# All work of border tiles five to eight in one conditional block over five engines

## The chip, the cores and the metric

The kernel runs on one core of one Trainium2 chip. The core has a matrix engine (TensorE, PE in the profile), a vector engine (VectorE, DVE), a scalar engine (ScalarE, ACT), a general engine (GpSimd, POOL) and an engine that mostly issues transfers (SyncE, SP). Each runs its own program in order; semaphores join them. Sixteen DMA engines move data. The metric is the device time of one execution in microseconds (us), lower is better; the number to be predicted is the median of several runs.

## What is computed

For 16 batches of 512 tokens with 512 features, the reference adds to `x` a small network over six normalised views of it, of which three take their scale and shift from tables by token, and three add a row per batch:

```python
h = _ln(x, pw_g[pathway_ids], pw_b[pathway_ids])
h = _ln(h, cp_g[compartment_ids], cp_b[compartment_ids])
t = _ln(x, tm_g[time_steps], tm_b[time_steps])
m = x + _mlp_ln(memory_state, ...)[:, None, :]
n = x + _mlp_ln(noise_state, ...)[:, None, :]
r = x + _mlp_ln(resource_state, ...)[:, None, :]
s = _ln(x, ms_g[scale_type], ms_b[scale_type])
cat = jnp.concatenate([w[0] * h, w[1] * t, w[2] * m, w[3] * n, w[4] * r, w[5] * s], axis=-1)
return x + _mlp_ln(cat, int_W1, int_b1, int_W2, int_b2, int_g, int_be)
```

## The kernel before

The tokens are sorted by the group of their table entries, so that most quarters of a window share one set of weights; the 8192 tokens are 16 windows of 512, each of four tiles of 128 rows. For a window, POOL gathers the rows of `x` (`gx`, into one of three buffers `xbs[0..2]`), the table rows (`gh`, `gc`) and an additive row per token (`ga`, from the DRAM table `rows_2`); ACT and DVE make the normalised rows (`xs`, `xe`, `xp`, `xm`, `nv`, `f1`, `fs`, `f2`, `fn`); DVE turns them (`tx`, `tv`, `th`), SP spreads the turned blocks (`sX`, `sV`, `sH`) into the operands `cats["X"]`, `cats["V"]`, `cats["H"]`; PE multiplies them by the weights (`lX`, `lV`, `lH` in the first windows). `lV.w.g` uses the weights `vs` that DVE updates in `bd.w.g` where the group changes. The buffers `xbs` go round: window 0 is in `xbs[2]` (`sh.0.j` adds a vector to its rows there), window 1 in `xbs[0]`, and `gx.2.j` gathers window 2 into `xbs[1]`.

Where a group's border falls inside a tile, a correction row is needed. Such rows are collected in border tiles of 128 rows, numbered k = 0 to 7, tiles one to four (k = 0 to 3) in the set `e0`, tiles five to eight (k = 4 to 7) in `e1`. How many rows there are is known only at run time, so every step of a border tile stands in a conditional of its own, on one engine: the tokens' numbers (`gt.1.j`, `tk.1`, `xa.1`), the gather of the rows (`gx.e1.j`), their sums (`xs.e1.j`, `xe.e1`, `xp.e1`, `xm.e1`), a gather of differences (`gr.e1.j`), normalisation and product (`nv.e1.j`, `mt.e1.j`), PE's transposition (`ey.k`), ACT's copy (`ez.k`), POOL's gather of what is added to (`ea.k`, tile `adde`), PE's product (`ex.k`), DVE's sum (`ee.k`) and SP's store to `rows_2` (`eo.k`). `rf.k` writes a filling row block to `rows_2` where the tile is empty, from `xbs[0]`. If the condition doesn't hold, the engine of a step walks over it, and raises the semaphores that its instructions would have raised; the other engines meet one branch.

The list `ORDER`, written out by hand, sets the order of all pieces up to the middle of window 2; each engine's program is the pieces' instructions on it in that order. Behind it the strings `WINDOW` and `LAST` do the same for the rest. In `ORDER` the pieces of tiles five to eight stand among those of tiles one to four and of window 1: the gathers and `rf.4` to `rf.7` early, `ey`, `ez`, `ea`, `ex`, `ee`, `eo` between `gx.2.3`, `xp.1`, `xm.1`, `lH.0.1` and `ga.0.1`.

Of the kernel before, what the change touches and what calls it, by code (L numbers as in the profile page):

```python
# [15 lines left out]
P = 128  # L16
# [5 lines left out]
    wk.1.3 wk.1.1 dk g4 wk.1.2 lt wk.1.0 h2.0 se ax pk cv sz g6 xs.0.0 scl fg wk.2.3 h2.2 he.0 sp.0.0 g5 h2.1  # L22
    pwi wk.2.2 xs.0.2 he.1 cg lo xt.0.0 he.2 lw bx lh by xt.0.1 gh.0.0 fl.3 xv.0.0 cw eh.1 xs.0.3 gc.0.0 xs.0.1
    xe.0 xt.0.3 wm.4 vd.0 kd xt.0.2 eh.0 wl.4 ac gh.0.2 xp.0 xm.0 tt nv.0.1 gt.0.0 eh.2 f1.0.0 nv.0.2 cs xv.0.3
    fs.0.0 gt.0.3 f1.0.2 dp gt.0.2 gt.0.1 cp fv.0.0 vt.0.1 fl.2 tk.0 xv.0.1 vt.0.2 va.1 cn vv.0.1 fl.4 tb wm.3
    nv.0.3 gc.0.2 gt.1.2 gt.1.0 vd.1 gt.1.3 va.0 ct ca wk.2.1 fl.1 wk.2.0 dc wm.2 do nv.0.0 gx.e0.0 vv.0.2
    gx.e0.1 rf.2 gx.e0.3 xv.0.2 sp.0.1 rf.6 rf.5 rf.1 xs.e0.0 f2.0.0 vt.0.0 vt.0.3 fs.0.2 f2.0.2 cm xs.e0.1 cr
    gt.1.1 gx.e0.2 lX.0.1 fp.0.0 fn.0.0 va.2 xs.e0.2 ht.0.0 gr.e0.0 rp1 gr.e0.1 xs.e0.3 rp.0 rp.1 rc.1 fv.0.2
    bd.0.0 bd.0.1 gh.0.1 vv.0.3 rc.0 wm.0 rf.0 lX.0.0 xe.e0 rf.7 tk.1 xp.e0 gx.e1.2 xm.e0 gx.e1.0 fp.0.2 rp2
    rf.4 hv.0.0 rf.3 fl.0 nv.e0.0 lX.0.2 mt.e0.0 gx.1.0 nv.e0.2 xa.0 nv.e0.1 mt.e0.1 ey.1 ey.0 vv.0.0 fn.0.2  # L30
    ez.0 wm.1 f1.0.1 gx.1.2 fs.0.1 gx.e1.1 gr.e0.2 ht.0.2 xa.1 hv.0.2 mt.e0.2 fv.0.1 xs.e1.1 ro.1 ro.0 ea.0
# [10 lines left out]
    fs.1.0 f1.1.1 fv.1.0 ha.0.1 hs.0.1 gc.1.1 ga.0.0 ha.0.3 ha.0.2 f2.1.0 tz.0.1 bd.1.1 ha.0.0 gx.2.0 sV.1.3
    sV.1.2 hs.0.2 kb.0.1 lV.1.0 hs.0.3 hs.0.0 tz.0.2 sX.1.3 tz.0.0 tz.0.3 gx.2.1 kb.0.0 sZ.0.1 xs.2.3 wq sh.0.3
    xs.2.0 xs.2.1 fs.1.1 sZ.0.0 sZ.0.2 ga.1.1 ga.1.2 sh.0.0 fp.1.0 fn.1.0 th.1.0 fv.1.1 zs.0.0 fp.1.1 lV.1.1
    m7.1.1.1 m7.1.0.1 q7.0.0.1 zs.0.1 zs.0.2 xe.2 q7.0.0.7 f2.1.1 fn.1.1 tx.2.2 th.1.1 gh.2.0 q7.0.0.2 xp.2
    kf.0.0 q7.0.0.5 q7.0.0.6 ku.0.0 sf.0.0 kz.0.3 kf.0.1 sZ.0.3 sp.1.2 kb.0.3 sp.1.3 bd.1.3 sh.1.2 tx.2.1
    q7.0.1.1 q7.0.1.2 sf.0.1 zs.0.3 zs.0.4 zs.0.5 lV.1.3 r1.1.1 kf.0.2 sf.0.2 tx.2.3 xm.2 nv.2.3 sl.0.0 ga.1.0
    sH.1.0 sH.1.3 nv.2.1 q7.0.1.5 tv.2.3 kf.0.3 sH.1.1 q7.0.0.3 nv.2.2 f1.2.0 q7.0.1.7 q7.0.0.4 tv.2.1 zs.0.6
    fs.2.0 nv.2.0 sh.1.1 zs.0.7 tv.2.2 sl.0.1 sf.0.3 sh.1.3 q7.0.1.6 m7.1.0.2 q7.0.1.4 q7.0.1.3 tv.2.0 fv.2.0
    r1.1.0 gh.2.1 lq.0.1 lq.0.0 sH.1.2 tx.2.0 bd.1.2 u1.1.1 u3.1.1 lV.1.2 u2.1.1 ku.0.1 m7.1.1.5 gc.2.0 sl.0.2  # L50
    sl.0.3 u1.1.0 u2.1.0 ga.1.3 lq.0.2 lq.0.3 f1.2.1 m7.1.1.4 m7.1.0.5 lv.0 m7.1.1.2 m7.1.0.6 r5.1.1 vd.2 f2.2.0
    sV.2.0 sp.2.0 lp.0 fp.2.0 fs.2.1 sp.2.1 fn.2.0 lb.0.0 lb.0.2 lb.0.3 po.0.0 gc.2.1 po.0.3 u4.1.0 u3.1.0
    fv.2.1 fp.2.1 r5.1.0 gx.3.0 r2.1.0 sV.2.1 sX.2.2 sV.2.3 sV.2.2 sX.2.0 m7.1.1.6 lb.0.1 u4.1.1 m7.1.0.7 gx.3.3
    bd.2.1 sX.2.1 r2.1.1 m7.1.0.3 m7.1.0.4 th.2.0 bd.2.0 f2.2.1 ha.1.0 r3.1.0 ha.1.1 m7.1.1.7 gh.2.2 gx.3.1
    gx.3.2 hs.1.1 po.0.1 fn.2.1 r3.1.1 th.2.1 gh.2.3 ha.1.3 m7.1.1.3 sh.1.0 sX.2.3 tz.1.1 hs.1.0 po.0.2 tz.1.0
    hs.1.3
# [38 lines left out]
def kernel(ctx: ExitStack, tc: tile.TileContext, a: dict, out: bass.AP):  # L95
# [190 lines left out]
    def x_sums(st, j):  # L286

        if st["w"] in BY_DVE:
            if "sums" not in st:
# [4 lines left out]
        if "sums" not in st:
            st["sums"] = small.tile([P, 3, NJ], F32, tag="sums", name="sums")
            if "n" in st:
                nc.vector.memset(st["sums"], 0.0)
# [1076 lines left out]
    def flip_extra(k):
        at_["px", k] = pt = ps.tile([P, NC, P], F32, tag="p", name=f"px{k}")
        r = ext[k // Q].pop(("r", k % Q))
        with tc.If(at_["some", 0][k] > 0):
            for c in range(NC):
                nc.tensor.transpose(pt[:, c], r[:, c * P : (c + 1) * P], ident)
# [8 lines left out]
    def extra(k):
        if ("pe", k) not in at_:
            at_["pe", k] = psum(f"pe{k}")  # L1390
        pe = at_["pe", k]
        with tc.If(at_["some", 0][k] > 0):
# [8 lines left out]

    def extra_end(k):
        with tc.If(at_["some", 1][k] > 0):
            nc.vector.tensor_add(at_["adde", k], at_["pe", k], at_["adde", k])
# [164 lines left out]
```

## Time and profile before

| | us |
|---|---|
| median of three runs (lowest, highest) | 915.65 (914.73, 918.04) |
| the profiled execution's own time | 914.96 |
| its span, first to last instruction | 913.2 |
| PE busy (share) | 884.2 (97%) |
| DVE busy (share) | 750.5 (82%) |
| POOL busy (share) | 676.7 (74%) |
| ACT busy (share) | 525.0 (57%) |

The profile has a page with shares, slices and groups, and views of the trace behind it. A row of the timeline has the start in us from the span's start, the busy time in us, the engine, the line of the code, the operation, what it writes and reads, a count of merged instructions, and in square brackets the idle time of the engine before it with what ended it. "PEq" is PE's sequencer (its branches and semaphores), "issue" means that nothing in the profile was waited for. A row of the waits has who waited for whom, the sum in us, the times, the longest. A row of the windows has a stretch, its length, the busy time of PE, PE's weight loads, DVE, ACT and POOL with the number of instructions, the granted clock of PE (1.00 is full), the share of the DMA engines, and GB/s. A row of SP shows when it issued transfers, not when they landed.

### The profile page before, as it was taken

Reading aid. Unit: us, or ns where it says so; the run is one execution under the profiler, and the core shown is the slowest. Engines: PE = TensorE matmul, PEld = TensorE weight load, DVE = VectorE, ACT = ScalarE, POOL = GpSimd, SP = SyncE. Lnnn points to the kernel's source line nnn. Section 1 sums busy time; section 2 is a strip of 40 time slices with the busy share of each in tenths; the row PEclk is TensorE's granted clock in tenths of the full one; section 3 lists DMA queues with packets and bytes.
Section 4 is the critical chain, followed back from the end, with each engine's and each line's share of the span. In section 5 each row is a group of like instructions: output and inputs, shape, how many; then the busy total and the mean of one; then the engine's idle time right before and its main releaser. Section 6 shows DMA issues by size and latency. Waiting matters only on the chain. (4 is left out here: it accounts for less than half of the span.)

```text
span 913.2 us, 13821 instructions
## 1 busy us (share of the span) xinstructions
PE 884.2 (97%) x3615; PEld 642.9 (70%) x3617; DVE 750.5 (82%) x1360; ACT 525.0 (57%) x1263; POOL 676.7 (74%) x726
## 2 busy tenths in 40 slices
PE   6898899999999999999999999999999999999996
...
GB/s 280 247 194 219 204 244 143 169 248 163 254 172 251 184 222 190 192 236 191 245 174 257 168 251 191 216 188 220 210 168 244 190 257 158 245 195 200 151 29 118
DMA packets 88239, 184.36 MB, mean 202 GB/s; under 512 B 24260, under 2 KB 24324, under 8 KB 88156
## 3 DMA queue, kind: packets, MB, share of 16 engines
...
q8 instruction: 30, 0.49, 0.2%
...
## 5 line engine op out<-in xcount | busy, mean ns | idle before, releaser
L417 PE MATMUL p<-vs,catV 128*128 128x512 f32 x512 | 229.7, 592 | 0.7 <-ACT junk L363 0.4
L417 PEld LDWEIGHTS p<-vs,catV 128*128 128x128 f32 x512 | 97.0, 190 | 99.2 <-issue 94.1
L389 ACT ACTIVATE pw<-pw,rsh 128x512 f32<-128x512 f32 x64 | 44.5, 718 | 136.7 <-POOL rsh L385 127.0
L465 PE MATMUL p<-wh__81,catH 128*128 128x256 f32 x480 | 113.4, 379 | 0.9 <-DVE catH L452 0.9
L465 PEld LDWEIGHTS p<-wh__81,catH 128*128 128x128 f32 x480 | 91.0, 190 | 14.0 <-DVE catH L452 1.7
L184 POOL DMA_INDIRECT xbs<-in_x,tok x64 | 74.1, 1158 | 34.8 <-DVE yb L647 18.1
L651 POOL DMA_INDIRECT out<-yb,tok x64 | 70.3, 1098 | 30.3 <-issue 18.3
L184 POOL DMA_INDIRECT cp<-cp_rows,i_cp x64 | 75.3, 1177 | 16.2 <-issue 15.4
L404 POOL TENSOR_TENSOR xbs<-xbs,rows 128x512 f32<-128x512 f32 x64 | 82.5, 1289 | 2.4 <-DMA cp<-cp_rows,i_cp 0.8
L184 POOL DMA_INDIRECT add<-rows,i_add x64 | 66.7, 1042 | 21.0 <-issue 11.7
L488 ACT ACTIVATE add<-add 128x512 f32<-128x512 f32 x64 | 39.9, 630 | 70.0 <-DVE add L485 69.4
L184 POOL DMA_INDIRECT pw<-in_pw,i_pw x64 | 65.1, 1018 | 19.3 <-DVE rH L210 7.5
L396 DVE SCALAR_TENSOR_TENSOR pw<-pw,sumsh,cp 128x512 f32<-128x512 f32 x60 | 55.7, 931 | 10.1 <-DMA cp<-cp_rows,i_cp 8.9
L638 POOL TENSOR_TENSOR rsy<-vey,mhalf 128x4 f32<-128x4 f32 (+1 forms) x16 | 22.0, 1376 | 53.2 <-DVE vey L633 53.2
L625 ACT ACTIVATE junk<-yb 128x512 bf16<-128x512 f32 x64 | 40.2, 629 | 34.4 <-DVE yb L589 16.6
L360 DVE SCALAR_TENSOR_TENSOR pw<-pw,rsx 128x512 f32<-128x512 f32 x64 | 57.5, 899 | 2.3
L385 POOL TENSOR_TENSOR rsh<-veh,mhalf 128x1 f32<-128x1 f32 x64 | 52.6, 824 | 8.4 <-DVE veh L381 6.8
L465 PEld LDWEIGHTS u<-wx__80,catX 128*128 128x128 f32 x240 | 45.6, 190 | 18.1 <-issue 10.0
L465 PE MATMUL u<-wt,catX 128*128 128x256 f32 x240 | 57.0, 381 | 0.9 <-DVE add L476 0.8
L465 PE MATMUL p<-wt,catH 128*128 128x256 f32 x240 | 56.7, 379 | 0.0
L465 PE MATMUL u<-wx__80,catX 128*128 128x256 f32 x240 | 56.5, 379 | 0.0
L465 PE MATMUL u<-wt,ss 128*128 128x256 f32 x240 | 56.4, 379 | 0.0
...
## 6 DMA issues: line engine op xcount, KB each, us to landing
catX<-rX SPq DMA_DIRECT2D x240, 64.0 KB
catV<-rV SPq DMA_DIRECT2D x240, 64.0 KB
catZ<-rZ SPq DMA_DIRECT2D x240, 64.0 KB
catH<-rH SPq DMA_DIRECT2D x240, 64.0 KB
...
```

The costliest lines, as they stand in the source:

```text
L184: nc.gpsimd.indirect_dma_start(dst, None, table, bass.IndirectOffsetOnAxis(ap=idx, axis=0), **kw)
L360: nc.vector.scalar_tensor_tensor(h, h, st["rs"][:, j : j + 1], pw[:, D:], ALU.mult, ALU.add)
L385: nc.gpsimd.tensor_tensor(rs, st.pop(("ve", j)), mhalf[:, :1], ALU.pow)
L389: nc.scalar.mul(pw[:, :D], pw[:, :D], st.pop(("rs", j)))
L396: nc.vector.scalar_tensor_tensor(pw[:, :D], pw[:, :D], st["sh", j][:, 1], cp, ALU.add, ALU.mult)
L404: nc.gpsimd.tensor_add(st["xb"][:, j, :], st["xb"][:, j, :], rows[:, 2, :])
L417: nc.tensor.matmul(st["p1", g], st["c" + blk][:, g, c, :], m[:, c, :], start=(blk == first and c == order[0]), stop=(blk == last and c == ...
L465: nc.tensor.matmul(dst, m[:, c], at_["half1"][k][:, c], start=(k == 1 and c == 0), stop=(c == NC - 1), skip_group_check=True)
L488: nc.scalar.activation(st["add", g], st["add", g], AF.Silu)
L625: nc.scalar.activation(junk, yb[:, j, :], AF.Square, accum_out=st["ssy"][:, j : j + 1])
L638: nc.gpsimd.tensor_tensor(st["rsy"][:, lo:hi], st["vey", lo], mhalf[:, lo:hi], ALU.pow)
L651: nc.gpsimd.indirect_dma_start(out_rows[j], bass.IndirectOffsetOnAxis(ap=tok[:, j, w : w + 1], axis=0), yb[:, j, :], None)
```

## The change

The pieces of tiles five to eight leave their places in `ORDER`. Two new pieces stand for them. `f5` loads the run-time condition for tile five into a register of each of the five engines. `ew`, behind `eo.2 eo.3`, holds all the work of the four tiles in one conditional block over the five engines; its other arm fills the four row blocks, which `rf.4` to `rf.7` did early before. Inside the block the gathers of differences go to `yb`, the normalised rows and the `adde` tiles to `xbs[1]`, the operand to `cats["Z"]`, and one PSUM tile each serves all `px` and all `pe`. The rest of the order is as it was. The core of the diff:

```diff
 ORDER = """
...
-    ... ey.6 bd.0.3 tx.1.0
-    wl.1 xs.1.3 ey.4 ee.2 hv.0.3 ex.3 ee.3 eo.2 eo.3 gr.e1.3 ea.4 xe.1 tx.1.3 mt.e1.3 sh.0.1 gr.e1.1 gh.1.2
-    gx.2.3 ea.7 ea.6 sh.0.2 ey.7 ez.7 ex.7 ea.5 ez.6 nv.e1.1 mt.e1.1 ey.5 sp.0.2 ez.5 xp.1 xm.1 ez.4 ex.4 ex.5
-    ee.5 ex.6 gc.1.3 wl.0 wl.3 gc.1.2 f1.1.3 nv.1.0 nv.1.1 lH.0.1 fs.1.3 lX.0.3 lV.0.3 lH.0.3 eo.5 f1.1.2 ee.6
-    fs.1.2 tv.1.0 ee.7 bd.0.2 f2.1.3 ee.4 eo.4 kz.0.2 lV.0.2 fv.1.2 tv.1.1 f2.1.2 nv.1.3 eo.6 gx.2.2 sX.1.2 eo.7
-    ga.0.1 lH.0.2 fv.1.3 kz.0.1 lH.0.0 ga.0.3 ...
+    ... bd.0.3 tx.1.0 wl.1 xs.1.3 ee.2 hv.0.3 ex.3 ee.3 eo.2 eo.3 ew xe.1 tx.1.3
+    sh.0.1 gh.1.2 gx.2.3 sh.0.2 sp.0.2 xp.1 xm.1 gc.1.3 wl.0 wl.3 gc.1.2 f1.1.3 nv.1.0 nv.1.1 lH.0.1 fs.1.3 lX.0.3
+    lV.0.3 lH.0.3 f1.1.2 fs.1.2 tv.1.0 bd.0.2 f2.1.3 kz.0.2 lV.0.2 fv.1.2 tv.1.1 f2.1.2 nv.1.3 gx.2.2 sX.1.2 ga.0.1
+    lH.0.2 fv.1.3 kz.0.1 lH.0.0 ga.0.3 ...
...
-                with tc.If(at_["some", 3][int(st["w"][1]) * Q + j] > 0):
+                with used(3, int(st["w"][1]) * Q + j):
...
     def rows_first(k):
         to, at = (rows_1, 0) if k == 0 else (rows_2, k - 1)
+        nc.sync.dma_start(to[NB1 + at * P : NB1 + (at + 1) * P, :], xbs[0][:, k % Q])
+
+    def first_of(k):
         with tc.If(at_["some", 4][k] < 1):
-            nc.sync.dma_start(to[NB1 + at * P : NB1 + (at + 1) * P, :], xbs[0][:, k % Q])
+            rows_first(k)
+
+    def used(e, k):
+        return nullcontext() if at_.get("whole") else tc.If(at_["some", e][k] > 0)
+
+    def rest_load():
+        _, at_["rest"] = nc.values_load_multi_w_load_instructions(
+            some[0:1, Q : Q + 1], engines=[mybir.EngineType.PE, mybir.EngineType.DVE, mybir.EngineType.Activation,
+                                           mybir.EngineType.Pool, mybir.EngineType.SP], min_val=0, max_val=2 * P,
+            skip_runtime_bounds_check_because="a comparison's result")
+
+    def rest_extras():
+        js = range(Q)
+        names = [f"gt.1.{j}" for j in js] + ["tk.1", "xa.1"] + [f"gx.e1.{j}" for j in js] + [f"xs.e1.{j}" for j in js]
+        names += ["xe.e1", "xp.e1", "xm.e1"]
+        for j in js:
+            names += [f"gr.e1.{j}", f"nv.e1.{j}", f"mt.e1.{j}", f"ey.{Q + j}", f"ez.{Q + j}"]
+        for j in js:
+            names += [f"ea.{Q + j}", f"ex.{Q + j}", f"ee.{Q + j}", f"eo.{Q + j}"]
+        with tc.If(at_["rest"][0] > 0) as cmp:
+            at_["whole"] = True
+            for n in names:
+                piece(n)
+            at_["whole"] = False
+        with cmp.Else():
+            for j in js:
+                rows_first(Q + j)
...
     def extra_add(k):
-        at_["adde", k] = gp.tile([P, D], F32, tag="add", name=f"adde{k}", bufs=4)
-        with tc.If(at_["some", 3][k] > 0):
+        at_["adde", k] = xbs[1][:, k % Q, :] if at_.get("whole") else gp.tile([P, D], F32, tag="add", name=f"adde{k}", bufs=4)
+        with used(3, k):
             gather(at_["adde", k], rows_1[: NB1 + (P if k else 0), :], add_x[:, k : k + 1])
...
-        "rp": rows_product, "rf": rows_first, ...
+        "rp": rows_product, "rf": first_of, "f5": rest_load, "ew": rest_extras, ...
```

What this moves is seen in each engine's program. A row has the line, the operation, what it writes and reads, the shape, and the semaphores that it waits for: DMASW0 to 7 for POOL's own gathers, DMAHW0 to 7 for the transfers of SP, and one for each engine. Line numbers of the change are its own.

POOL before, from `gh.1.2` (`pw1_2`) and `gx.2.3` (the gather into `xbs1`) on, with the first of the skipped gathers of tiles five to eight behind them:

```order
L184 DMA pw1_2_1414<-in_pw,i_pw_106 128x1024 [waits DMASW6_49,PE_49,Activation_49]
L184 DMA xbs1_90<-in_x,tok_105 128x512 [waits DMASW7_49]
L1399 COMPARE_AND_BRANCH
L184 DMA adde7_1417<-rows_1_76,i_x_539 128x512 [waits DMAHW4_49,DMAHW6_49,DMAHW2_49,DMAHW7_49,DMASW0_49,DVE_49]
L1399 UNCONDITIONAL_BRANCH
L1399 ISA [waits DMASW0_49]
L1399 UNCONDITIONAL_BRANCH
```

The gather `gx.2.3` waits for one earlier gather (DMASW7) there. Two more such skipped gathers, the add of `sh.0.2` and a row of branches stand between it and `xp.1`.

POOL after, from the end of the block's other arm on; `L399` are `sh.0.1` and `sh.0.2`, `rsx_1435` is `xp.1`:

```order
L1378 ISA [waits Pool_49,DMASW4_49,DMASW5_49,DMASW3_49,DMASW6_49,DMASW2_49,DMASW7_49,DMASW1_49,DMASW0_49]
L1378 UNCONDITIONAL_BRANCH
L256 UNCONDITIONAL_BRANCH
L399 TENSOR_TENSOR xbs2_91<-xbs2_91,rows_97 128x512 [waits DMAHW6_49,DMASW1_49]
L179 DMA pw1_2_1426<-in_pw,i_pw_106 128x1024 [waits DMASW0_49,DMASW1_49,PE_49,Activation_49]
L179 DMA xbs1_90<-in_x,tok_105 128x512 [waits DMAHW1_49,DMASW2_49,DVE_49]
L399 TENSOR_TENSOR xbs2_91<-xbs2_91,rows_97 128x512
L308 TENSOR_TENSOR rsx_1435<-vea_1422,mhalf_103 128x4 [waits DVE_49]
L179 DMA cp1_3_1439<-cp_rows_75,i_cp_107 128x512 [waits DMASW4_49,DMASW3_49]
L179 DMA cp1_2_1443<-cp_rows_75,i_cp_107 128x512 [waits DMASW5_49,DMASW4_49]
```

The skipped gathers are gone from between `gx.2.3` and `xp.1`, the arm has one row that waits for all eight queues of gathers, and `gx.2.3` has come to wait for DMAHW1, DMASW2 and DVE.

SP before, in the early part of the program, two of the fills `rf.4` to `rf.7`, each in its own conditional:

```order
L1360 COMPARE_AND_BRANCH
L1361 DMA rows_2_78<-xbs0_89 128x512 [waits DMAHW2_49]
L1360 UNCONDITIONAL_BRANCH
L1360 UNCONDITIONAL_BRANCH [waits DMAHW2_49]
L1360 COMPARE_AND_BRANCH
L1361 DMA rows_2_78<-xbs0_89 128x512 [waits DMAHW3_49]
L1360 UNCONDITIONAL_BRANCH
L1360 UNCONDITIONAL_BRANCH [waits DMAHW3_49]
```

SP after: the same stores from `xbs0` stand as `L1355` in the block's other arm, behind the block's branch, which itself follows the store `eo.3`; `L1434` are the stores `eo.4` to `eo.7` from `xbs1` of the arm with the work.

```order
L1378 COMPARE_AND_BRANCH
L1434 DMA rows_2_78<-xbs1_90 128x512 [waits DMAHW6_49,DVE_49]
L1434 DMA rows_2_78<-xbs1_90 128x512 [waits DMAHW7_49,DVE_49]
L1434 DMA rows_2_78<-xbs1_90 128x512 [waits DMAHW0_49,DVE_49]
L1434 DMA rows_2_78<-xbs1_90 128x512 [waits DMAHW1_49,DVE_49]
L1378 UNCONDITIONAL_BRANCH
L1355 DMA rows_2_78<-xbs0_89 128x512 [waits DMAHW6_49,DMASW3_49]
L1355 DMA rows_2_78<-xbs0_89 128x512 [waits DMAHW7_49,DMASW3_49]
L1355 DMA rows_2_78<-xbs0_89 128x512 [waits DMAHW0_49,DMASW4_49]
L1355 DMA rows_2_78<-xbs0_89 128x512 [waits DMAHW1_49,DMASW2_49]
L1378 UNCONDITIONAL_BRANCH
L256 UNCONDITIONAL_BRANCH
```

The fills have moved from the early part to this place, ahead of the spreads of window 1, and both arms raise DMAHW6, 7, 0 and 1 in this order.

PE before, the last two of the six conditionals between `ex.3` and the product `lH.0.1` (`p1_0_1<-wh`):

```order
L1392 COMPARE_AND_BRANCH
L1394 MATMUL pe5_1473<-wt_83,catX_93 128x512 [waits DVE_49,PE_49,Activation_49]
L1394 MATMUL pe5_1473<-wt_83,catX_93 128x512 x3
L1392 UNCONDITIONAL_BRANCH
L1392 UNCONDITIONAL_BRANCH [waits PE_49]
L1392 COMPARE_AND_BRANCH
L1394 MATMUL pe6_1481<-wt_83,catX_93 128x512 [waits DVE_49,PE_49,Activation_49]
L1394 MATMUL pe6_1481<-wt_83,catX_93 128x512 x3
L1392 UNCONDITIONAL_BRANCH
L1392 UNCONDITIONAL_BRANCH [waits PE_49]
L417 MATMUL p1_0_1_990<-wh__81,catH_94 128x512 [waits DVE_49,Activation_49]
```

PE after, the end of the block's arm with the work, its other arm (`L1378` with a wait for PE itself), and `lH.0.1`:

```order
L1419 MATMUL pe4_1390<-wt_83,catZ_96 128x512 [waits DVE_49]
L1419 MATMUL pe4_1390<-wt_83,catZ_96 128x512 x3
L1419 MATMUL pe4_1390<-wt_83,catZ_96 128x512 [waits DVE_49,Activation_49]
L1419 MATMUL pe4_1390<-wt_83,catZ_96 128x512 x3
L1378 UNCONDITIONAL_BRANCH
L1378 UNCONDITIONAL_BRANCH [waits PE_49]
L256 UNCONDITIONAL_BRANCH
L412 MATMUL p1_0_1_985<-wh__81,catH_94 128x512 [waits DVE_49,Activation_49]
```

The six conditionals, and two ahead of `ex.3`, are gone; one block stands in their place.

More of the change, by code (lines that the diff above doesn't have):

```diff
@@ L1 @@
-from contextlib import ExitStack
+from contextlib import ExitStack, nullcontext
 import concourse.bass as bass
@@ L21 @@
 ORDER = """
[L22 to L31, printed above, removed]
@@ L42 @@
[L42 to L51, printed above, removed]
@@ L52 @@
[L52 to L56, printed above, removed]
+    wk.1.3 wk.1.1 dk g4 wk.1.2 lt wk.1.0 h2.0 se ax pk cv sz g6 xs.0.0 scl fg wk.2.3 h2.2 he.0 sp.0.0 g5 h2.1 pwi
@@ new lines @@
+    wk.2.2 xs.0.2 he.1 cg lo xt.0.0 he.2 lw bx lh by xt.0.1 gh.0.0 fl.3 xv.0.0 cw eh.1 xs.0.3 gc.0.0 xs.0.1 xe.0
+    xt.0.3 wm.4 vd.0 kd xt.0.2 eh.0 wl.4 ac gh.0.2 xp.0 xm.0 tt nv.0.1 gt.0.0 eh.2 f1.0.0 nv.0.2 cs xv.0.3 fs.0.0
+    gt.0.3 f1.0.2 dp gt.0.2 gt.0.1 cp fv.0.0 vt.0.1 fl.2 tk.0 xv.0.1 vt.0.2 va.1 cn vv.0.1 fl.4 f5 tb wm.3 nv.0.3
+    gc.0.2 vd.1 va.0 ct ca wk.2.1 fl.1 wk.2.0 dc wm.2 do nv.0.0 gx.e0.0 vv.0.2 gx.e0.1 rf.2 gx.e0.3 xv.0.2 sp.0.1 rf.1
+    xs.e0.0 f2.0.0 vt.0.0 vt.0.3 fs.0.2 f2.0.2 cm xs.e0.1 cr gx.e0.2 lX.0.1 fp.0.0 fn.0.0 va.2 xs.e0.2 ht.0.0 gr.e0.0
@@ new lines @@
+    rp1 gr.e0.1 xs.e0.3 rp.0 rp.1 rc.1 fv.0.2 bd.0.0 bd.0.1 gh.0.1 vv.0.3 rc.0 wm.0 rf.0 lX.0.0 xe.e0 xp.e0 xm.e0
+    fp.0.2 rp2 hv.0.0 rf.3 fl.0 nv.e0.0 lX.0.2 mt.e0.0 gx.1.0 nv.e0.2 xa.0 nv.e0.1 mt.e0.1 ey.1 ey.0 vv.0.0 fn.0.2
+    ez.0 wm.1 f1.0.1 gx.1.2 fs.0.1 gr.e0.2 ht.0.2 hv.0.2 mt.e0.2 fv.0.1 ro.1 ro.0 ea.0 wl.2 ex.0 gc.0.1 xs.1.0 ez.1
+    ey.2 gh.0.3 wb lV.0.0 f2.0.1 lV.0.1 gr.e0.3 ee.0 fp.0.1 ar nv.e0.3 mt.e0.3 fn.0.1 ht.0.1 f1.0.3 ez.2 xs.1.2 eo.0
+    ey.3 ex.1 gx.1.3 gx.1.1 gc.0.3 fs.0.3 f2.0.3 ea.1 ea.3 gh.1.3 fv.0.3 ex.2 tx.1.2 sp.0.3 fp.0.3 ez.3 xs.1.1 hv.0.1
@@ new lines @@
+    ha.0.1 hs.0.1 gc.1.1 ga.0.0 ha.0.3 ha.0.2 f2.1.0 tz.0.1 bd.1.1 ha.0.0 gx.2.0 sV.1.3 sV.1.2 hs.0.2 kb.0.1 lV.1.0
+    hs.0.3 hs.0.0 tz.0.2 sX.1.3 tz.0.0 tz.0.3 gx.2.1 kb.0.0 sZ.0.1 xs.2.3 wq sh.0.3 xs.2.0 xs.2.1 fs.1.1 sZ.0.0 sZ.0.2
+    ga.1.1 ga.1.2 sh.0.0 fp.1.0 fn.1.0 th.1.0 fv.1.1 zs.0.0 fp.1.1 lV.1.1 m7.1.1.1 m7.1.0.1 q7.0.0.1 zs.0.1 zs.0.2
+    xe.2 q7.0.0.7 f2.1.1 fn.1.1 tx.2.2 th.1.1 gh.2.0 q7.0.0.2 xp.2 kf.0.0 q7.0.0.5 q7.0.0.6 ku.0.0 sf.0.0 kz.0.3
+    kf.0.1 sZ.0.3 sp.1.2 kb.0.3 sp.1.3 bd.1.3 sh.1.2 tx.2.1 q7.0.1.1 q7.0.1.2 sf.0.1 zs.0.3 zs.0.4 zs.0.5 lV.1.3
@@ new lines @@
+    r1.1.1 kf.0.2 sf.0.2 tx.2.3 xm.2 nv.2.3 sl.0.0 ga.1.0 sH.1.0 sH.1.3 nv.2.1 q7.0.1.5 tv.2.3 kf.0.3 sH.1.1 q7.0.0.3
+    nv.2.2 f1.2.0 q7.0.1.7 q7.0.0.4 tv.2.1 zs.0.6 fs.2.0 nv.2.0 sh.1.1 zs.0.7 tv.2.2 sl.0.1 sf.0.3 sh.1.3 q7.0.1.6
+    m7.1.0.2 q7.0.1.4 q7.0.1.3 tv.2.0 fv.2.0 r1.1.0 gh.2.1 lq.0.1 lq.0.0 sH.1.2 tx.2.0 bd.1.2 u1.1.1 u3.1.1 lV.1.2
+    u2.1.1 ku.0.1 m7.1.1.5 gc.2.0 sl.0.2 sl.0.3 u1.1.0 u2.1.0 ga.1.3 lq.0.2 lq.0.3 f1.2.1 m7.1.1.4 m7.1.0.5 lv.0
+    m7.1.1.2 m7.1.0.6 r5.1.1 vd.2 f2.2.0 sV.2.0 sp.2.0 lp.0 fp.2.0 fs.2.1 sp.2.1 fn.2.0 lb.0.0 lb.0.2 lb.0.3 po.0.0
```

44 lines of the change are left out of this document (23 added, 21 removed).

## The prediction

> **What bounds the kernel now.** I read the engine shares and slices first, then TensorE's waits from 45 to 250 us, then each engine's timeline around 100 to 135 us, where the moved work stood.
>
> ```profile
> span 913.2 us, 13821 instructions
> PE 884.2 (97%) x3615; PEld 642.9 (70%) x3617; DVE 750.5 (82%) x1360; ACT 525.0 (57%) x1263; POOL 676.7 (74%) x726
> PE   6898899999999999999999999999999999999996
> ...
> PE p L417 <- PEq L1392: 2.5, 1, 2.5
> PE px L1379 <- DVE sums L297: 1.4, 1, 1.4
> ...
> PE pq_1b L559 <- DVE yb L578: 0.9, 1, 0.9
> PE pe L1394 <- PEq L1377: 0.8, 1, 0.8
> ```
>
> TensorE (PE) is the bound: 884.2 of 913.2 us, and full from the fourth slice to the last but one. So a microsecond that PE loses early stays lost, and one that it gains early stays won, unless a wait behind it takes it back. Two of its waits belong to the change: 2.5 us at L1392 and 0.8 us at L1377, where PE's own sequencer (PEq) walks over untaken Ifs of tiles five to eight.
>
> ```profile
> 103.81 3.67 PE L1394 MATMUL pe<-wt,catZ 128*128 128x512 f32 x8 [0.84 <-PEq L1377]
> 109.95 3.67 PE L417 MATMUL p<-wh__81,catH 128*128 128x512 f32 x8 [2.47 <-PEq L1392]
> ...
> 123.98 3.60 PE L417 MATMUL p<-vs,catV 128*128 128x512 f32 x8
> ...
> 131.06 3.60 PE L417 MATMUL p<-wh__81,catH 128*128 128x512 f32 x8
> 134.71 7.03 PE L417 MATMUL p<-vs,catV 128*128 128x512 f32 x16
> ```
>
> After 109.95 PE runs without a break, through `lV.0.2` (123.98) to `lV.1.0` (134.71), whose operand `vs` VectorE (DVE) releases in `bd.1.1`.
>
> **What is removed.** In this run the gathers of the border-sum tiles show how many tiles have rows: the trace has four (`adde`), so tiles five to eight are empty and the new block goes to its other arm. Six untaken Ifs stand in the 2.47 us gap, 0.41 each; one block remains, so I take 2.0 off. The two in the 0.84 gap go whole. PE is then 2.8 ahead, at `lV.0.2` by 121.1 instead of 123.98. The untaken Ifs on the other engines lie beside PE's dense work from 109.95 on, which hides them: nothing, and 0.4 each if that cover were gone. The five register loads of `f5` come early, where PE's list of waits shows none of the loads of the same kind that stand there already; nothing, or up to the 2.8 of lead. The early fills leave the gathers before 75 us more room, at best the 1.4 us of `px`. All such early terms, of either sign, end in the same idle time of PE below, and count only if that wait fails to come.
>
> **What is added: a wait.** The fills of tiles five to eight leave SP's early stretch and stand behind the store `eo.3`. POOL's gather `gx.2.3` (third POOL operation behind the block) now waits for the semaphore of the fourth fill, because the block's taken arm stores from the buffer `xbs[1]` that this gather overwrites; both arms share the semaphore. Before, it waited for no store. Behind it in POOL's queue stand `sh.0.2`, then `xp.1` (`rsx`), for which DVE's `xm.1`, and by it the whole front of window 1, waits.
>
> ```profile
> 100.17 1.00 POOL L184 DMA_INDIRECT adde<-rows,i_x  x1 [0.17 <-issue]
> 101.93 1.49 POOL L404 TENSOR_TENSOR xbs<-xbs,rows 128x512 f32<-128x512 f32 x1 [0.76 <-DMA cp<-cp_rows,i_cp]
> 103.74 1.06 POOL L184 DMA_INDIRECT pw<-in_pw,i_pw  x1 [0.33 <-PEq L1377]
> 105.11 1.00 POOL L184 DMA_INDIRECT xbs<-in_x,tok  x1 [0.30 <-issue]
> 106.49 1.27 POOL L404 TENSOR_TENSOR xbs<-xbs,rows 128x512 f32<-128x512 f32 x1 [0.38 <-DMA pre<-diff_rows,i_x]
> 108.36 1.04 POOL L313 TENSOR_TENSOR rsx<-vea,mhalf 128x4 f32<-128x4 f32 x1 [0.61 <-DVE vea L309]
> ...
> 111.04 1.10 POOL L184 DMA_INDIRECT cp<-cp_rows,i_cp  x1 [0.30 <-DMA rows<-adde]
> ...
> 114.67 1.40 POOL L184 DMA_INDIRECT add<-rows,i_add  x1 [1.09 <-DMA catX<-rX]
> ```
>
> *When the fills land.* SP's rows and the stages around the four copies `rows<-rows`, the nearest like thing (four stores of 240 KB on one queue):
>
> ```profile
> 74.72 0.35 SPq L1355 DMA_DIRECT2D rows<-rows  x1
> ...
> 76.45 0.98 SPq L1356 DMA_DIRECT2D rows<-rows  x1
> 106.51 2.04 SPq L1409 DMA_DIRECT2D rows<-adde  x2
> 80.00:81.00 1.00, 1.00 (x8) 0.60 (x7) 0.96 (x3) 0.44 (x1) 1.00 (x1) 1.00 0.96 299
> 81.00:82.00 1.00, 0.91 (x8) 0.67 (x7) 0.96 (x2) 0.49 (x2) 0.69 (x2) 1.00 0.78 221
> 103.00:111.00 8.00, 4.72 (x11) 2.04 (x12) 6.82 (x12) 4.58 (x10) 5.81 (x6) 1.00 0.67 222
> 111.00:120.00 9.00, 9.00 (x23) 3.98 (x22) 5.63 (x11) 5.78 (x14) 5.99 (x6) 1.00 0.79 216
> ```
>
> The two stores of 106.51 span 2.04 with the second's issue of about 0.33, so `eo.3` went out near 108.2; with `ex.3` 0.84 earlier it goes out at 107.4, and half a microsecond later, at 107.9, the first fill. *Low end*: POOL's row at 111.04 was released by that store, so 256 KB land within 2.8 us; the fourth fill, issued some 1.2 after the first (0.35 to 0.4 each), lands at 107.9 + 1.2 + 2.8 = 111.9. *High end*: at a share of 0.67 the engines moved 222 GB/s, 331 at full; the fills (1.05 MB) getting only the third that is free, 109 GB/s, need 9.6 us: 117.5. *Taken*: the copies were issued from 74.72, and the share falls from 0.96 to 0.78 at 81, 6.4 us on; so 114.3.
>
> *What follows.* `gx.2.3` starts at 114.4 instead of 105.11. `rsx` follows at the old spacing without its wait for `vea` (106.49 + 1.27 - 105.11 = 2.65), and ends at 114.4 + 2.65 + 0.1 + 1.04 = 118.2 instead of 109.40: 8.8 late. In the block's other arm POOL also waits for all its gathers to land, so `sh.0.1` follows the last `adde`, landed by 105.84 (DVE's row below reads it); this lies under the wait for the fills.
>
> ```profile
> 105.84 0.65 DVE L1404 TENSOR_TENSOR adde<-pe,adde 128x512 f32<-128x512 f32 x1
> ...
> 109.44 0.16 DVE L324 TENSOR_TENSOR nmx<-sums,rsx 128x4 f32<-128x4 f32 x1 [0.55 <-POOL rsx L313]
> ...
> 119.03 0.71 DVE L210 STREAM_TRANSPOSE rH<-pw 128x512 f32<-128x512 f32 x1 [2.15 <-ACT pw L389]
> ...
> 133.18 0.70 DVE L210 STREAM_TRANSPOSE rZ<-add 128x512 f32<-128x512 f32 x1
> ...
> 134.69 0.69 DVE L485 TENSOR_TENSOR add<-p,add 128x512 f32<-128x512 f32 x1 [0.81 <-DMA catV<-rV]
> ```
>
> From `xm.1` (109.44) DVE's chain runs to `bd.1.1`, which stands between the last two of these rows: 133.88 at the earliest, 24.5 after `rsx`'s end, with one long wait, at 119.03, which goes back through ACT's `pw` to POOL's `rsh` and the 1.09 wait of `add` at 114.67 for SP's spread; SP's untaken stores stood ahead of that spread. I take 1.0 off for it (0 to 1.1). So `lV.1.0` may start at 118.2 + 24.5 - 1.0 = 141.7 instead of 134.71: **PE loses 7.0** (4.6 at the low end; 10.2 at the high). The slack before was 134.71 - 133.88 = 0.8. PE's 2.8 lead becomes idle time there: about 1.7 before `lV.0.2` (its `bd.0.2` stands in the same delayed queue of DVE) and 8 before `lV.1.0`.
>
> **The clock.** An idle stretch can also halve the granted clock:
>
> ```profile
> 42.00:44.00 2.00, 0.56 (x8) 0.00 (x0) 1.90 (x8) 2.00 (x5) 1.62 (x6) 1.00 0.96 313
> 44.00:46.00 2.00, 1.37 (x10) 0.32 (x10) 1.39 (x4) 1.39 (x4) 1.84 (x5) 0.52 1.02 400
> ...
> 52.00:54.00 2.00, 2.00 (x5) 0.34 (x3) 1.76 (x12) 1.94 (x8) 1.80 (x3) 0.50 0.84 219
> 54.00:56.00 2.00, 2.00 (x13) 1.00 (x12) 1.25 (x2) 2.00 (x6) 1.69 (x2) 0.92 0.58 217
> ...
> 44.63 0.20 PE L1018 MATMUL pst<-of_seg,room 14*14 14x4 f32 x2 [2.07 <-POOL of_seg L1011]
> ```
>
> After a gap of 2.07 us the clock stood at half for about 10 us; after the 0.84 and 2.47 us gaps it stayed at 1.00 (the row 103 to 111). Ten microseconds of dense products at half speed cost 5; no drop costs 0. I take the middle, **2.5**, since `lV.1.0` starts 16 dense products of 128x512, while 44 to 54 held small ones.
>
> [...]
>
> **Sum**, against the profiled execution's own 914.96 us (913.2 of span, 1.8 around it; the median of the runs, 915.65, is 0.7 above): 914.96 + 7.0 + 2.5 = 924.5.
>
> **The rivals.**
> 1. *The fills land early, the clock holds*: 4.6 or less and no drop. If the fills cost nothing at all, POOL's drain still puts `sh.0.1` at 105.3, `gx.2.3` at 108.3 and `rsx`'s end at 112.1, 2.7 late; less 1.8 of slack and savings `lV.1.0` is 0.9 late. So 915.9 to 919.6, within 0.5%. For it: 2.8 us for one store. Against: four of them on engines that are two thirds busy.
> 2. *Faster*: PE keeps its lead if `rsx` ends by 121.1 + 10.7 - 23.5 = 108.3 (10.7 being PE's work from `lV.0.2` to `lV.1.0`), and gains anything only if it ends by 111.2, so if `gx.2.3` starts before 107.4. Then up to 2.8 come off: 912.2. Against: `eo.3` itself goes out only at 107.4 and the fills behind it. It decides if POOL doesn't in fact wait for them.
> 3. *Stall without the half clock*: 922.0. For it: 1.00 through the gaps at 103 and 110. Against: these were a third as long.
> 4. *The high end*: fills squeezed by gathers, and a long half clock: 914.96 + 10.2 + 3.4 = 928.6.
>
> **How the numbers follow.** My forecast with rivals 3 and 4 (one mechanism, other sizes) has 0.77, split 0.5, 0.17 and 0.1; rival 1 has 0.19, rival 2 has 0.04. A difference of 0.5%, 4.6 us, is about what a measurement of this kernel can tell from none: slower means over 920.2, faster under 911.1. The range runs from 917.5, inside rival 1, to 928.5, the end of the bounds; about 0.15 lies below it and 0.05 above.
>
> **What would show it.** Right: POOL's `xbs<-in_x,tok` of 105.11 stands near 114 with an idle time of several microseconds put down to a DMA of `rows`; `rsx` near 117; PE shows a gap of about 8 us before `p<-vs,catV` x16, and PEclk 0.50 for some microseconds behind it; PEq's 2.5 and 0.8 us are gone or 0.5 in all. Wrong: that gather starts before 107.4 (then rival 2), PE's gap is there but the span is unchanged (then PE wasn't the bound behind it), or the fills' landing comes before 111.

## The result, and the profile after

The changed kernel takes 926.06 us (median of 12 runs, 923.41 to 931.71) beside 919.53 for the kernel before (12 runs, 914.73 to 923.44; the three runs of the table above are among them): a ratio of **1.0080, 95% interval 1.0054 to 1.0106**. In a second comparison (after_again, below) it was 1.0064 (1.0044 to 1.0083). So it is slower by some 6 to 7 us. The kernel before against itself gave 0.9994 (0.9978 to 1.0011). The profile of the kernel before is of an execution of 914.96 us, below its medians in the comparisons (916.7 to 920.2), so that a loss read between profiles comes out too large and a gain too small; one execution of the kernel before of 2153.0 us and one of slot_first of 3309.24 us count in no ratio.

The page after, with the shares and PE's slices; the profiled execution took 924.12 us:

```profile
span 922.3 us, 13718 instructions
PE 888.4 (96%) x3615; PEld 644.1 (70%) x3617; DVE 745.2 (81%) x1349; ACT 524.4 (57%) x1263; POOL 673.0 (73%) x725
...
PE   6999978999999999999999999999999999999996
```

PE is the bound as before, and full from the eighth slice on. PE's waits from 40 to 250 us after:

```profile
PE p L412 <- DMA catV<-rV: 3.2, 1, 3.2
PE pq_0a L554 <- DMA catZ<-rZ: 2.5, 1, 2.5
PE p L412 <- DVEq L256: 2.3, 2, 2.0
...
PE p L412 <- PE pe L1419: 0.3, 1, 0.3
```

The two waits for the skipped conditionals (2.5 and 0.8) are gone; 0.3 is left of them. Three new ones stand in their place, 7.7 us in all. POOL's timeline after shows where they come from:

```profile
98.75 0.99 POOL L179 DMA_INDIRECT adde<-rows,i_x  x1 [0.17 <-POOLq L1378]
104.54 1.26 POOL L399 TENSOR_TENSOR xbs<-xbs,rows 128x512 f32<-128x512 f32 x1 [4.80 <-DMA pw<-in_pw,i_pw]
105.97 0.96 POOL L179 DMA_INDIRECT pw<-in_pw,i_pw  x1 [0.16 <-ACT w L1457]
115.53 0.96 POOL L179 DMA_INDIRECT xbs<-in_x,tok  x1 [8.61 <-DMA rows<-xbs]
116.52 1.27 POOL L399 TENSOR_TENSOR xbs<-xbs,rows 128x512 f32<-128x512 f32 x1
117.74 1.04 POOL L308 TENSOR_TENSOR rsx<-vea,mhalf 128x4 f32<-128x4 f32 x1
```

The gather `gx.2.3` stands idle for 8.61 us until a transfer `rows<-xbs`, a fill, has landed. `rsx` ends at 118.78 instead of 109.40, 9.4 late. The 4.80 ahead of `sh.0.1` is the block's own wait for POOL's gathers. PE's timeline after:

```profile
106.55 3.67 PE L412 MATMUL p<-wh__81,catH 128*128 128x512 f32 x8 [0.34 <-PE pe L1419]
...
122.76 3.67 PE L412 MATMUL p<-vs,catV 128*128 128x512 f32 x8 [2.02 <-DVEq L256]
126.27 7.25 PE L412 MATMUL p<-wh__81,catH 128*128 128x512 f32 x16
...
136.90 5.10 PE L412 MATMUL p<-vs,catV 128*128 128x512 f32 x8 [3.18 <-DMA catV<-rV]
142.40 3.67 PE L412 MATMUL p<-vs,catV 128*128 128x512 f32 x8 [0.40 <-ACT pq_0b L528]
...
152.00 1.10 PE L554 MATMUL pq_0a<-w,catZ 128*128 128x256 f32 x4 [2.47 <-DMA catZ<-rZ]
```

`lH.0.1` starts at 106.55 instead of 109.95, 3.4 ahead. `lV.0.2` is then 1.2 ahead, `lV.1.0` 2.2 behind, and the first product with `catZ` stands at 152.00. Before, PE's timeline had it at

```profile
145.03 1.03 PE L559 MATMUL pq_0a<-w,catZ 128*128 128x256 f32 x4
```

so PE is 7.0 late there; in the kernel before it came to this product without a wait. The windows after (stretch, length, busy times, then clock, DMA share, GB/s) show the clock:

```profile
135.00:140.00 5.00, 3.10 (x4) 1.46 (x5) 4.46 (x8) 1.94 (x6) 4.07 (x5) 0.66 1.06 260
140.00:145.00 5.00, 4.61 (x11) 1.82 (x10) 4.58 (x8) 3.79 (x8) 2.45 (x3) 1.00 1.04 225
...
150.00:155.00 5.00, 2.99 (x9) 2.28 (x10) 2.12 (x6) 2.93 (x7) 2.46 (x4) 0.84 0.41 97
155.00:160.00 5.00, 4.95 (x19) 4.10 (x20) 1.58 (x3) 1.61 (x4) 4.81 (x6) 0.81 0.67 170
```

It fell twice, behind the 3.18 gap and behind the 2.47 one. A stretch at half clock reads 0.50 (52 to 54 us of the kernel before), so a row of 5 us with t of them at half shows 1 - t/10; by this estimate the first drop lasted 3.4 us (0.66) and the second 3.5 (0.84 and 0.81). The delay at the end of the span is 9.1 us (922.3 against 913.2).

### The profile page after: what moved, and what is told of

Same layout as the page of the kernel before. It is cut to its first block, busy times and chain, and to the rows that moved or that the text cites. A ratio compares the mean times of both kernels' runs of the same rounds, so it can differ in the third digit from the quotient of the medians.

```text
span 922.3 us, 13718 instructions
## 1 busy us (share of the span) xinstructions
PE 888.4 (96%) x3615; PEld 644.1 (70%) x3617; DVE 745.2 (81%) x1349; ACT 524.4 (57%) x1263; POOL 673.0 (73%) x725
## 5 line engine op out<-in xcount | busy, mean ns | idle before, releaser
L179 POOL DMA_INDIRECT xbs<-in_x,tok x64 | 73.7, 1151 | 43.5 <-DVE yb L642 18.1
L399 POOL TENSOR_TENSOR xbs<-xbs,rows 128x512 f32<-128x512 f32 x64 | 82.2, 1284 | 6.1 <-DMA pw<-in_pw,i_pw 4.8
L391 DVE SCALAR_TENSOR_TENSOR pw<-pw,sumsh,cp 128x512 f32<-128x512 f32 x60 | 53.2, 888 | 10.7 <-issue 6.7
L325 ACT ACTIVATE xm<-xbs,nmx,rsx 128x512 f32<-128x512 f32 x64 | 48.9, 807 | 20.9 <-DVE nmx L319 13.1
L460 PEld LDWEIGHTS u<-wx__80,catX 128*128 128x128 f32 x240 | 45.6, 190 | 18.1 <-issue 12.0
```

Source lines behind the costliest of these rows:

```text
L179: nc.gpsimd.indirect_dma_start(dst, None, table, bass.IndirectOffsetOnAxis(ap=idx, axis=0), **kw)
L391: nc.vector.scalar_tensor_tensor(pw[:, :D], pw[:, :D], st["sh", j][:, 1], cp, ALU.add, ALU.mult)
L399: nc.gpsimd.tensor_add(st["xb"][:, j, :], st["xb"][:, j, :], rows[:, 2, :])
L460: nc.tensor.matmul(dst, m[:, c], at_["half1"][k][:, c], start=(k == 1 and c == 0), stop=(c == NC - 1), skip_group_check=True)
```

## The experiments

Theory: `gx.2.3` waits for the fourth fill, and `rsx` and the front of window 1 stand behind it. Rivals: the block itself (its branch on five engines, POOL's wait for all its gathers); the late transfers, whoever waits for them. Ratios are to the kernel before on the same chip. Times of PE's first product with `catZ` are compared with `rsx`'s end in each kernel's own profile, because the profiles of nearly equal programs differ by up to 4 us at 90 us already.

**after_again**, the changed kernel as it is.

> The changed kernel once more, as a measure for the three beside it. Both theories: 0.5 to 1.1% slower than before (5 to 10 us), with the gather xbs<-in_x,tok idle for about 8.6 us until the landing of rows<-xbs, as in its first profile.

Ratio 1.0064 (1.0044 to 1.0083). The gather's idle time was 9.14 us.

**early_fills**: the block stays, the fills leave it.

```diff
-        with cmp.Else():
-            for j in js:
-                rows_first(Q + j)
...
-    ... rf.2 gx.e0.3 xv.0.2 sp.0.1 rf.1
+    ... rf.2 gx.e0.3 xv.0.2 sp.0.1 rf.6 rf.5 rf.1
...
+    ... rf.7 xp.e0 ... rp2 rf.4 hv.0.0 ...
```

> The block stays, but its other arm is empty; the four fills go back to their early places, each in its own conditional. Theory (the wait for the fills holds POOL's queue): the block's drain still makes POOL wait for its gathers, so the gather xbs<-in_x,tok starts near 107.3 and rsx ends near 110.8 instead of 118.8; the products with catZ, which began at 152.1 in the change, begin near 144; time from 3 below to 1 above the kernel before. Rival (the block itself, its drain and its branch on five engines, costs the time): still 5 us or more above. Rival (late transfers): as the theory.

Ratio 1.0004 (0.9984 to 1.0024). POOL's timeline of early_fills:

```profile
109.27 1.26 POOL L399 TENSOR_TENSOR xbs<-xbs,rows 128x512 f32<-128x512 f32 x1 [4.79 <-DMA pw<-in_pw,i_pw]
...
113.06 0.96 POOL L179 DMA_INDIRECT xbs<-in_x,tok  x1 [1.41 <-SPq L1378]
...
115.27 1.04 POOL L308 TENSOR_TENSOR rsx<-vea,mhalf 128x4 f32<-128x4 f32 x1
```

The block's wait is there (4.79), the 8.6 are gone, and with them the loss in the timed runs. 1.41 are left, put down to SP's branch at the block (`SPq L1378`). The times stand some 5 us later than expected since this execution had lost 4 us ahead of 90 us, and for these 1.41. The first product with `catZ` begins at 149.20, 32.9 after `rsx`'s end. The block itself isn't the cause.

**adde_own**: the fills stay late, but the `adde` tiles leave `xbs[1]`.

```diff
-        at_["adde", k] = xbs[1][:, k % Q, :] if at_.get("whole") else gp.tile([P, D], F32, tag="add", name=f"adde{k}", bufs=4)
+        at_["adde", k] = gp.tile([P, D], F32, tag="add", name=f"adde{k}", bufs=4)
```

> The fills stay late in the block's other arm, but the adde tiles of the arm with the work are the four tiles of their own as before, not xbs[1], so the gather into xbs[1] waits for no store. Theory: that gather starts near 107.3, rsx ends near 110.8, fills still land near 115; time from 3 below to 1 above the kernel before. Rival (late transfers, whoever waits for them, take the time from gathers and spreads): 3 us or more above. Rival (the block itself): 5 us or more above.

Ratio 1.0011 (0.9993 to 1.0029). POOL's timeline of adde_own, and PE's:

```profile
105.64 1.27 POOL L399 TENSOR_TENSOR xbs<-xbs,rows 128x512 f32<-128x512 f32 x1 [5.00 <-DMA pw<-in_pw,i_pw]
...
108.54 0.96 POOL L179 DMA_INDIRECT xbs<-in_x,tok  x1 [0.51 <-issue]
...
110.75 1.04 POOL L308 TENSOR_TENSOR rsx<-vea,mhalf 128x4 f32<-128x4 f32 x1
```

```profile
144.93 2.04 PE L554 MATMUL pq_0a<-w,catZ 128*128 128x256 f32 x4 [2.37 <-DMA catZ<-rZ]
```

The transfers go out as late as in the change (SP issues the fills from 108.52, there from 107.75), nobody on the path waits for them, and the loss is gone: late transfers by themselves cost nothing here that can be measured (1.0011). `rsx` ends at 111.79, 2.4 later than before; about 0.6 of that this execution had lost by 95 us, the rest is the price of the block; the first product with `catZ` begins 33.1 later.

**gather_behind**: the wait stays, the two gathers stand further back.

```diff
-    sh.0.1 gh.1.2 gx.2.3 sh.0.2 ... nv.1.3 gx.2.2 sX.1.2 ... fp.1.3 sX.1.1
+    sh.0.1 gh.1.2 sh.0.2 ... nv.1.3 sX.1.2 ... fp.1.3 gx.2.3 gx.2.2 sX.1.1
```

> The wait stays, but the two gathers of window 2 into xbs[1] (gx.2.3, gx.2.2) stand behind fp.1.3 in the order, so that sh.0.2, xp.1 and the cp gathers don't queue behind them. Theory: rsx ends near 109.5 though the fills land near 115; add<-rows at 115 as before; time from 3 below to 1 above the kernel before. Rival (the block itself): 5 us or more above. Rival (late transfers): 3 us or more above.

Ratio 0.9999 (0.9982 to 1.0017). POOL's timeline of gather_behind:

```profile
110.34 1.04 POOL L308 TENSOR_TENSOR rsx<-vea,mhalf 128x4 f32<-128x4 f32 x1
...
119.82 1.29 POOL L179 DMA_INDIRECT add<-rows,i_add  x1 [5.92 <-DMA catX<-rX]
```

What stood behind the gather was the cost. But `add<-rows` (`ga.0.1`), which reads `rows_2` and so needs the fills in any case, now waits 5.92 and starts at 119.82, not at 115 as expected: the next late link. (The row names the transfer that landed last.) In this profile PE comes to the product with `catZ` at 149.77, having been 2.2 late at 95 us; that is 2.6 lost on the way, which the timed ratio doesn't show.

**wide_fills**: each fill moves two row blocks, in turn.

```diff
-                rows_first(Q + j)
+                at = NB1 + min(Q + j - 1, 2 * Q - 3) * P
+                nc.sync.dma_start(rows_2[at : at + 2 * P, :].rearrange("(t p) f -> p t f", p=P), xbs[0][:, :2])
```

> Each fill of the block's other arm writes two row blocks (512 KB) instead of one, and since they overlap each waits for the one ahead; still only filling rows are written, some twice. Theory (the time is the landing of the fourth fill plus a fixed chain: rsx ends 4.1 us after it, the products with catZ begin 33 us after that): at 3.5 to 5 us a fill the fourth lands at 122 to 128, rsx ends at 126 to 132, the products begin at 159 to 165 instead of 145 before; 14 to 20 us above the kernel before, and some 2 us more for the half clock. Rival (the block's drain): as the change, 5 to 10 us above.

Ratio 1.0125 (1.0103 to 1.0148), 11.5 us. POOL's timeline of wide_fills, and PE's:

```profile
123.40 0.96 POOL L179 DMA_INDIRECT xbs<-in_x,tok  x1 [17.05 <-DMA rows<-xbs]
...
125.60 1.04 POOL L308 TENSOR_TENSOR rsx<-vea,mhalf 128x4 f32<-128x4 f32 x1
```

```profile
130.62 6.32 PE L412 MATMUL p<-vs,catV 128*128 128x512 f32 x8 [10.20 <-DVEq L256]
...
159.62 1.82 PE L554 MATMUL pq_0a<-w,catZ 128*128 128x256 f32 x4 [2.39 <-DMA catZ<-rZ]
```

The chain holds: the gather starts at 123.40, `rsx` ends at 126.64, and the product begins at 159.62, 33.0 later, all at the low end of what was expected. The gather starts 7.9 us later than in the change, and the product 7.6. The timed loss, 11.5 us (9.4 to 13.6), is under the 14 to 20 forecast, though the product is 14.6 later than in the profile of the kernel before; a part of that difference is that profile's (see the result), the rest is open.

**slot_first**: `adde` tiles in reverse order in `xbs[1]`.

```diff
-        at_["adde", k] = xbs[1][:, k % Q, :] if ...
+        at_["adde", k] = xbs[1][:, Q - 1 - k % Q, :] if ...
```

> The adde tiles of the arm with the work take the four places of xbs[1] in reverse, so the gather of the fourth place waits for the first fill's semaphore instead of the fourth's. Theory: that gather starts when the first fill lands, about 1.9 us sooner than in the change (113 against 115), rsx ends near 117, the products with catZ begin near 150; 5 us above the kernel before instead of 7 (0.3 to 0.8%). Rival (all four fills have to land whoever waits): as the change.

Ratio 1.0046 (1.0027 to 1.0065), within what was expected, but its interval reaches that of the change. **slot_first_look** is the same kernel once more, for its profile:

> slot_first once more, for an undisturbed profile. Theory: the gather xbs<-in_x,tok starts about 1.9 us sooner after the block than in the change, when the first fill has landed (7 us idle instead of 8.6 to 9.1), and the products with catZ begin 33 us after the end of rsx. Rival: it starts with the fourth fill's landing.

POOL's timeline of slot_first_look:

```profile
107.63 0.96 POOL L179 DMA_INDIRECT pw<-in_pw,i_pw  x1 [0.16 <-issue]
114.87 0.96 POOL L179 DMA_INDIRECT xbs<-in_x,tok  x1 [6.28 <-DMA rows<-xbs]
```

The idle time is 6.28 instead of 8.61 and 9.14, and the gather starts 5.6 after SP issued the first fill (109.25) instead of 7.8 and 7.7: it waits for the fill whose semaphore it shares, not for all four. The first product with `catZ` begins at 150.96, 32.8 after `rsx`'s end. The one execution itself took 923.95 us, so the 2.3 to 2.9 us are seen at the wait and only weakly in the time.

**awake**: products in PE's idle time, whose result the next ones overwrite.

```diff
-    ... lV.1.0 ... lV.1.1 ...
+    ... wu.lV.1.0.0 wu.lV.1.0.1 wu.lV.1.0.2 wu.lV.1.0.3 ... lV.1.0 ... wu.lV.1.1.0 wu.lV.1.1.1 wu.lV.1.1.2 lV.1.1 ...
```

> The changed kernel with seven products whose result is overwritten, four ahead of lV.1.0 and three ahead of lV.1.1, in PE's idle time there. Theory (of the loss some 2 to 3 us are the half clock after these idle times): clock stays at 1.00 through lV.1.0 and lV.1.1, and the time is 4 to 6 us above the kernel before instead of 6 to 9. Rival (the half clock falls where the next wait, for catZ, hides it): the time is as the change.

Ratio 1.0050 (1.0031 to 1.0069). PE's timeline of awake (L421 are the added products):

```profile
133.57 3.60 PE L421 MATMUL awake_lV<-wt 128*128 128x512 f32 x8
137.00 3.60 PE L412 MATMUL awake_lV<-vs,catV 128*128 128x512 f32 x8
140.43 2.74 PE L421 MATMUL awake_lV<-wt 128*128 128x512 f32 x6
143.01 3.60 PE L412 MATMUL awake_lV<-vs,catV 128*128 128x512 f32 x8
...
151.77 1.10 PE L554 MATMUL pq_0a<-w,catZ 128*128 128x256 f32 x4 [1.71 <-ACT junk L360]
```

`lV.1.0` takes 3.60 instead of 5.10, at full clock (1.00), and the product with `catZ` starts at 151.77, where it did in the change (152.00). So what the clock cost at `lV.1.0` was hidden by the wait behind it: here the rival was right. The timed ratio, 4.6 us (2.8 to 6.3), is what the theory forecast, but its interval reaches that of the change, so the time decides nothing. In this profile the clock stays at 1.00 behind `catZ` too.

**shifts_ahead**: adde_own, and POOL's two adds ahead of the block.

```diff
-    ... hv.0.3 ex.3 ee.3 eo.2 eo.3 ew xe.1 tx.1.3 sh.0.1 gh.1.2 gx.2.3 sh.0.2 sp.0.2 xp.1 ...
+    ... hv.0.3 sh.0.1 sh.0.2 ex.3 ee.3 eo.2 eo.3 ew xe.1 tx.1.3 gh.1.2 gx.2.3 sp.0.2 xp.1 ...
```

> adde_own, and the two adds sh.0.1 and sh.0.2 stand ahead of the block, so that POOL does them in the time in which the block makes it wait for its gathers. Theory: rsx ends near 109.5 instead of 111.8 in adde_own, the products with catZ begin near 142.5, PE keeps its lead over the skipped Ifs: 1 to 3 us below the kernel before, 2 below adde_own. Rival (the waits behind, for DVE at yb, take the lead back): within 0.2% of the kernel before.

Ratio 0.9995 (0.9981 to 1.0009). POOL's timeline of shifts_ahead, and PE's:

```profile
108.56 1.04 POOL L308 TENSOR_TENSOR rsx<-vea,mhalf 128x4 f32<-128x4 f32 x1
...
118.27 0.94 POOL L179 DMA_INDIRECT add<-rows,i_add  x1 [4.70 <-DMA catX<-rX]
```

```profile
136.78 5.37 PE L412 MATMUL p<-vs,catV 128*128 128x512 f32 x8 [2.13 <-ACT pq_0b L528]
...
146.27 1.10 PE L554 MATMUL pq_0a<-w,catZ 128*128 128x256 f32 x4 [0.67 <-ACT junk L360]
```

`rsx` ends at 109.60, as expected, but the product with `catZ` comes at 146.27, not 142.5: `add<-rows` waits 4.70 (the row names the transfer that landed last; the fills it needs went out just ahead of those). Neither the theory's gain nor the rival's wait for `yb`: a third thing, the late fills' other reader.

**all_ahead**: shifts_ahead with the fills early, as in early_fills.

> shifts_ahead with the fills at their early places too, so that neither the gather into xbs[1] nor the gather add<-rows behind it waits for late fills. Theory (in shifts_ahead the wait for the fills moved to add<-rows, which started at 118.3): add<-rows starts near 114.5, rsx ends near 109.5, the products with catZ begin near 142.5; 1 to 3 us below the kernel before (0.997 to 0.999). Rival (waits behind, for DVE at yb, take back what PE gains): within 0.1% of the kernel before.

Ratio **0.9942 (0.9920 to 0.9964)**. POOL's timeline of all_ahead, and PE's:

```profile
111.33 1.04 POOL L308 TENSOR_TENSOR rsx<-vea,mhalf 128x4 f32<-128x4 f32 x1
...
116.65 0.94 POOL L179 DMA_INDIRECT add<-rows,i_add  x1 [0.30 <-issue]
```

```profile
145.56 1.10 PE L554 MATMUL pq_0a<-w,catZ 128*128 128x256 f32 x4 [1.25 <-ACT junk L360]
```

`add<-rows` no longer waits. This version beats both kernels. Its profile shows less of the gain: this execution was 2.0 late at 95 us and 0.5 late at the product, so it won about 1.5 from there on.

**before_again** and **all_ahead_2**, to see whether that is chance.

> The kernel before against itself, as a measure of what a comparison of this kernel shows by chance: ratio within 0.998 to 1.002, and a profile whose PE is within 4 us of the first one at 90 us, as the profiles of the other versions were.

> all_ahead once more, since its gain of 0.6% is more than its profile explains. If the gain is what its PE shows from 90 us on (1.5 us): 0.997 to 0.999. If there is a gain before 90 us that its one profile happened not to have: again 0.992 to 0.996.

0.9994 (0.9978 to 1.0011) and 0.9942 (0.9923 to 0.9961). The profile of before_again was 1.6 late at 95 us and 2.7 at the end. The gain of all_ahead came again; both comparisons ran on one chip. The profile of all_ahead_2 was 4.2 late at 95 us and 2.2 late at the end, again 1.9 won, so some 3.5 us of the timed 5.3 don't show between the profiles. Those of all_ahead are of executions above their medians (916.33 and 917.36 us beside 914.26 and 914.88), while that of the kernel before is below its own; what sets an execution's time ahead of 95 us stays open.

## Why the prediction was right, and where not

- **The wait for the fills**: right. The gather started at 115.53 (forecast 114.4), put down to `rows<-xbs`; `rsx` began at 117.74 (near 117). From the four copies I took 6.4 us from the first issue to the landing; it was 7.8 (107.75 to 115.53). early_fills, adde_own and gather_behind each take one leg of it away, and each takes the loss with it; wide_fills makes it longer.
- **PE's lead**: 3.4 instead of 2.8 (0.2 of it was there at 95 us), and it went into idle time, as forecast; 2.02 at `lV.0.2` (1.7 forecast). A lead of 2.6 in adde_own ended in a wait for `catZ` of 2.37.
- **Where it ends**: wrong in place. The step was that `lV.1.0` waits for `bd.1.1`, with 0.8 of slack and some 8 us idle. The timeline merges `lV.1.0` and `lV.1.1` in one row of before, and I took the release of one for that of the other. `lV.1.0` was released by the spread `catV<-rV` at 136.90, 18.1 after `rsx`'s end (in after_again and slot_first_look by DVE's `pw`, 17.4 after it), so before it had about 7 us of slack (134.71 less 109.40 + 18.1). `lV.1.1` is the one that needs `bd.1.1`: it waited 0.40 in the change, put down to ACT at `pq_0b`, and 3.00 in gather_behind, put down to DVE's branch at L256. The gap forecast at 8 us was 3.18; PE's idle time stands in three gaps instead (2.02, 3.18, 2.47). The wait that ends last is at the products with `catZ`, 33.0 to 33.2 after `rsx`'s end in the change, adde_own and wide_fills, against 35.6 in the kernel before: 2.4 of slack.
- **The loss of PE**: 7.0 forecast, 7.0 in the profile of the change at that product, by errors that cancelled: the delay of `rsx` was 9.4 (8.8 forecast), less 2.4 of slack, where I took off 0.8 of slack and 1.0 of a wait gone. That wait is gone (`add<-rows` stands 0.31 idle in the change), but it isn't seen separately, and can be a part of the 2.4.
- **The half clock**: that it falls was right; its place and the 2.5 were not. The 1.5 us it cost at `lV.1.0` were hidden by the next wait (awake). Behind `catZ` PE's delay grew from 7.0 to 9.0 in the first profile. At 164.13 us of the kernel before it is down to 8.0, since PE had waited 0.90 for `yb` there before and doesn't in the change. In after_again and awake, where the clock doesn't fall behind `catZ`, the delay goes from 6.1 to 5.3 and from 6.7 to 5.9. So the half clock behind `catZ` cost about 1.8 that lasts in the first profile, and nothing in the other two. No gap of PE from 95 to 160 us of the change was longer than 3.18; the clock fell behind that one and behind 2.47, and stayed at 1.00 behind 2.02.
- **The sum**: 9.5 forecast, 9.1 between the two profiles, of which 8.0 are there at 164 us and the rest comes behind 300 us, where before_again, too, falls back from 1.7 to 2.7; 7.3 (4.9 to 9.7) by the first ratio, 5.9 (4.0 to 7.6) by the second. The term that was too large is the clock. The time itself, 926.06 for a forecast of 924.5, is nearer than the difference is: the kernel before, too, took longer in these runs than in the three that I started from (919.53 instead of 915.65), and that is luck.
- **Rival 1**, the block's own drain without the fills' wait: its working (`rsx` at 112.1, 0.9 us lost) is what adde_own shows (111.8, ratio 1.0011); it wasn't what the change did. **Rival 2** needed POOL not to wait; it waited. **Rival 3** had the clock at full; it fell. **Rival 4** had the landing at 117.5 and a long half clock; the gather started at 115.53, and the drops lasted 3.4 and 3.5 us. No run shows the 3.4 us that its sum, and with it the upper end of the range, takes as the cost of the half clock: in wide_fills eight products behind 10.20 us of idle time took 6.32 instead of 3.60, 2.7 more, and in the change about 1.8 lasted.
